# Earlier starting turns for three groups of cross-attention and spline scores inside a delta-rule loop

## The chip, the core and the metric

The kernel runs on one core of a Trainium2 chip. A core has a matrix engine (TensorE, "PE" in the profile, with its weight loads as "PEld"), three elementwise engines (VectorE "DVE", ScalarE "ACT", GpSimd "POOL"), a queue that issues transfers (SyncE "SP") and 16 transfer engines. Each engine works through its own queue in order; a program's semaphores tie the queues together. The metric is the device time of one execution in microseconds, and the figure quoted for a kernel is the median of its runs.

## What is computed

The reference is a decoder of four blocks, each made of a mixing layer, a cross-attention and a feed-forward layer, with a layer norm after every one of the twelve. The input `x` has 16 sequences of 128 tokens with 256 features. Only the first block matters here. Cut to what is needed:

```python
# layer 0: gated delta rule, 16 heads of 128; S is the state of a head
err = S @ k_t - v_t
S   = a_t * S - b_t * outer(err, k_t)
o_t = S @ q_t                      # then norm, gate, projection Wo
x = _layernorm(x + o @ Wo)

# layer 1: attention over a context, with an additive mask
x = _layernorm(x + softmax(q @ k.T / 16 + mask) @ v)

# layer 2: a spline for each token, chosen by scores of signs
xf = layernorm(x) * gamma + beta
cluster_scores = sign(xf) @ cluster_sigs.T        # best cluster, then best tile in it
tile_idx = argmax(where(in_cluster, tile_scores, -inf))
tile_min, tile_max = min / max over ALL tokens that chose a tile
x = _layernorm(x + x + spline(xf[tile_idx], tile_min, tile_max))
```

Layers 1 and 2 work on each sequence by itself, except for the last step of layer 2, which needs the extremes over all tokens. In the kernel the attention of layer 1 is taken over the tokens of `x` itself with the mask added, in line with how the reference calls it.

## The kernel before

The 16 sequences form four groups of four (`NG = 4`, a group is g = 0 to 3). A copy of `x` with features on the partitions (`xT`) and one with tokens on them (`X`) stay on the chip.

The delta rule (`s0`, from line 564) is computed in a chunked form, one unit for one head of one group, so 64 units, u = 16 g + h. A unit has two generators: `s0_inverse` (A: projections of k and q, taps of a short convolution, the decay matrix, the inverse of a triangular matrix by many 32 x 32 matmuls) and `s0_values` (B: projections of v and the gate, the output of the head, its norm, its share of the output projection). `weave` (line 299) interleaves them by hand: in turn n it walks through a fixed list of entries, and an entry (A, lag) or (B, lag) runs the next piece of unit n - lag. Two entries of the list, (C, 0), run the next piece of a third generator, `extra`. They stand seventh and thirteenth of the list, ahead of the entry that projects k and q for the turn's own unit. There are 64 units and the largest lag is 9, so there are turns 0 to 72. From turn 64 on fewer and fewer units are left and the turns get shorter. While this runs, every compute instruction is held to the order in which the program lists it on its engine (`Ordered`, line 312); transfers on SP are not.

A group is finished by unit 16 g + 15. Its output projection, the addition to `X` and the norm's moments come in turn 16 g + 23, and the norm itself and the new `xT` in turn 16 g + 24 (`s0_values`, lines 941 to 955, and `finish_in_turns`). These two turns carry more work than the others; they are called finishing turns here. For group 3 they are turns 71 and 72, the last ones.

`extra` is `s12_early` (line 965). For groups 0, 1 and 2 it runs layer 1 (`s1_group`, line 977) and the scores of layer 2 (`s2_scores`, line 1065). Both yield after each piece, 13 and 13 times, so that one group takes 13 turns at two pieces a turn. `s12_early` counts pieces and holds a group back until its starting turn. The pieces of a group in order:

- two turns of q and k projections (`qk`, four pieces of two 128 x 512 matmuls), one turn of the v projection (two pieces)
- scores with the mask (`sc`, VectorE) and the exponentials (ScalarE), then the transposes of the weights and the product with v, the addition to `X` and layer 1's norm
- `s2_scores`, nearly without TensorE: moments, `xfsg` (normalised features and signs, 128 x 1024, on VectorE, ScalarE and GpSimd), the reductions `ts`, `cs`, `best`, `oh`, `xs`, and the running extremes `run`

When the weave is over, `s0` runs whatever `extra` still has (lines 651 and 652). Then `s12_late` (line 1145) does layer 1 and the scores for group 3, and the rest of layer 2 for all groups. That part is not held to program order.

Two facts tie the groups together. The buffers of these pieces exist once: `wide` (line 981 and line 1069) holds `qk` first and `xfsg` after, so that a group's `qk` can be written only when `xs` of the group before has been read. And `mask` exists once, so that a group's mask is loaded after `sc` of the group before.

Of the kernel before, what the change touches and what calls it, by code (L numbers as in the profile page):

```python
# [326 lines left out]
class Decoder:  # L327
# [637 lines left out]
    def s12_early(self, wk, w, held):  # L965

        pieces = 0
        for g, turn in enumerate((40, 56, 68)):
            while pieces < 2 * turn:
                pieces += 1  # L970
                yield
            for part in (self.s1_group(wk, w, g), self.s2_scores(wk, held, g)):
                for _ in part:
                    pieces += 1
                    yield
# [1608 lines left out]
```

## Time and profile before

| | |
|---|---|
| median of 3 runs | 3933.04 us (3927.8 to 3938.19) |
| span of the profiled execution | 3927.2 us |
| TensorE busy | 3561.2 us, 91% |
| VectorE / ScalarE / GpSimd busy | 64% / 53% / 50% |
| chain that ended last | 73% on TensorE, 12% VectorE, 6% ScalarE, 5% GpSimd |
| mean granted TensorE clock | 0.950 |

The profile gives a time for the span alone, from the first to the last instruction; it lies 5.8 us below the median of the runs and 0.6 us below their fastest. Times in the trace count from the start of the span. The delta rule with its 64 units fills the first 1370 us or so, and the end of layer 2 comes about 1490. A turn can be told in the trace by ScalarE's first pass over the k projection (`acck<-bankA`), of which there is one in each of turns 0 to 63: turn 22 starts at 431.30, turn 38 at 747.19, turn 54 at 1071.51 and turn 62 at 1241.89 by this mark. Since the two entries of `extra` stand ahead of the mark in their turn, the stretch from mark n to mark n + 1 holds the pieces of turn n + 1.

How to read such a page: a busy share says how much of the span an engine worked, not whether it set the pace. What set the pace is read from the chain of waits and from stretches of equal content that are held against each other.

### The profile page before, as it was taken

The numbers are of one execution on the slowest core, as the hardware profiler recorded it, in microseconds if no ns is written. First come the engines' busy times: TensorE is split into PE (matmuls) and PEld (weight loads), VectorE is DVE, ScalarE is ACT, GpSimd is POOL, SyncE is SP. The second block draws the span as 40 slices with busy tenths as digits, with TensorE's granted clock in tenths as the row PEclk, the third lists the DMA queues.
The fourth block names the chain that finished last, engine by engine and source line by source line (L and its number), as shares of the span: only waits on it lengthen the run. The fifth ranks groups of instructions, "written<-read, shape, count | busy, mean of one in ns | idle before, by whom it ended". The sixth has DMA issues, their size and how long they took to land.

```text
span 3927.2 us, 96527 instructions
## 1 busy us (share of the span) xinstructions
PE 3561.2 (91%) x39282; PEld 2164.1 (55%) x39282; DVE 2528.1 (64%) x5489; ACT 2076.7 (53%) x4583; POOL 1965.7 (50%) x2227
## 2 busy tenths in 40 slices
PE   6999999999999837798989998988999999999896
PEld 4666566666666524565545664665455454555453
DVE  3776667768767565566235556755666677666697
ACT  2666666666666513343115444544656565566386
POOL 1444444435434316652125552343886666676567
PEclk8999999999999968899979998998999999999898
DMA  2111111111111101100010003111111111111221
GB/s 88 35 38 37 35 37 38 36 36 37 37 35 33 37 0 47 42 12 16 1 57 30 27 24 110 52 48 46 36 42 37 36 42 36 41 38 40 74 68 33
DMA packets 120841, 156.47 MB, mean 40 GB/s; under 512 B 15632, under 2 KB 79888, under 8 KB 120016
## 3 DMA queue, kind: packets, MB, share of 16 engines
q1 hardware_dynamic: 114544, 143.59, 12.0%
q8 instruction: 311, 5.10, 0.6%
q10 hardware_dynamic: 5712, 5.19, 0.4%
q0 software_dynamic: 144, 1.52, 0.1%
q14 instruction: 130, 1.06, 0.1%
HBM read 131.64 MB, written 2.10 MB: 34 GB/s over the span
## 4 chain that ended last, share of the span: by engine, by line
PE 73%; DVE 12%; ACT 6%; POOL 5%; issue 3%; DMA 1%; SPq 0%; ACTq 0%; POOLq 0%; DVEq 0%
PE bankA L324 39%; PE bankB L324 20%; PE bankC L324 8%; PE bankA L465 3%; DVE npad L324 2%; PE bankB L465 2%; ACT accq L324 1%; ACT ot L324 1%; ACT gT L324 1%; POOL var L324 1%; DVE X L324 1%; DVE ln_st L324 1%; POOL t L324 1%; DVE t L324 0%; DVE accq L324 0%
## 5 line engine op out<-in xcount | busy, mean ns | idle before, releaser
L324 PE MATMUL bankA<-xT,wzx 128*128 128x512 f32 x1024 | 458.1, 600 | 0.0
L324 DVE SCALAR_TENSOR_TENSOR acc<-bankA,half,acc 128x508 f32<-128x508 f32 (+2 forms) x384 | 285.2, 743 | 167.2 <-ACT acc L324 158.2
L324 POOL TENSOR_TENSOR m<-m,gm 128x512 f32<-128x512 f32 x256 | 317.9, 1277 | 48.0 <-ACT m L324 48.0
L324 PEld LDWEIGHTS bankA<-xT,wzx 128*128 128x128 f32 x1024 | 190.1, 191 | 226.6 <-issue 188.4
L324 POOL TENSOR_TENSOR eb<-eb,c_tri_s 128x512 f32<-128x512 f32 x64 | 81.2, 1269 | 371.5 <-ACT eb L324 371.5
L324 POOL TENSOR_TENSOR gT<-yx,sz 128x512 f32<-128x512 f32 x128 | 160.5, 1275 | 211.4 <-DVE yx L324 211.4
L324 PE MATMUL bankA<-xT,wkq 128*128 128x512 f32 x512 | 259.1, 631 | 0.0
L324 PE MATMUL bankA<-xT,wvg 128*128 128x512 f32 x512 | 247.5, 606 | 0.1
L324 PE MATMUL bankC<-gT,wo 128*128 128x512 f32 x512 | 231.9, 596 | 2.7 <-POOL gT L324 2.7
L324 DVE TENSOR_REDUCE npad<-bankA 128x2 f32<-128x512 f32 (+1 forms) x320 | 196.9, 681 | 37.6 <-PE bankA L324 29.0
L324 ACT ACTIVATE m<-bankA 128x512 f32<-128x512 f32 x256 | 132.1, 604 | 157.4 <-PE bankA L324 157.4
L324 ACT ACTIVATE e<-bankA 128x512 f32<-128x512 f32 x320 | 165.2, 603 | 82.2 <-PE bankA L324 81.7
L324 POOL TENSOR_TENSOR sq<-sq,s 128x512 f32<-128x512 f32 x124 | 157.5, 1271 | 56.6 <-ACT s L324 51.9
L324 POOL TENSOR_SCALAR rs_ve<-o_mv 128x4 f32<-128x4 f32 x64 | 31.5, 492 | 298.9 <-DVE o_mv L324 289.6
L324 DVE SCALAR_TENSOR_TENSOR vT<-th,accv 128x512 f32<-128x512 f32 x64 | 45.4, 710 | 182.1 <-ACT th L324 182.1
L324 PEld LDWEIGHTS bankB<-y,tt 32*32 32x32 f32 x8192 | 87.5, 107 | 129.1 <-issue 93.7
L324 DVE SCALAR_TENSOR_TENSOR yx<-xs,cols,bankB 128x512 f32<-128x512 f32 x128 | 95.0, 747 | 90.2 <-PE bankB L324 84.5
L324 DVE SCALAR_TENSOR_TENSOR acck<-bankA,half_cols,acck 128x508 f32<-128x508 f32 (+2 forms) x192 | 142.5, 742 | 11.3 <-ACT acck L324 4.8
L324 PEld LDWEIGHTS bankC<-gT,wo 128*128 128x128 f32 x512 | 93.4, 192 | 98.4 <-issue 93.5
L324 DVE SCALAR_TENSOR_TENSOR accq<-bankA,half_cols,accq 128x508 f32<-128x508 f32 (+2 forms) x192 | 142.2, 740 | 4.5
L324 ACT ACTIVATE acc<-bankA,half 128x512 f32<-128x512 f32 x128 | 100.7, 786 | 80.0 <-PE bankA L324 80.0
L324 DVE SCALAR_TENSOR_TENSOR accv<-bankA,half_cols,accv 128x508 f32<-128x508 f32 (+2 forms) x192 | 140.0, 729 | 4.5
(528 smaller groups left out, 9375.9 us busy)
## 6 DMA issues: line engine op xcount, KB each, us to landing
wzx<-in_s_wzx SPq DMA_DIRECT2D x64, 512.0 KB
up<-cums SPq DMA_DIRECT2D x1152, 2.0 KB
wkq<-in_s_w SPq DMA_DIRECT2D x64, 256.0 KB
wvg<-in_s_w SPq DMA_DIRECT2D x64, 256.0 KB
wo<-in_s_wo SPq DMA_DIRECT2D x64, 128.0 KB
sw<-qraw SPq DMA_DIRECT2D x64, 128.0 KB
eo<-in_ctx_eo SPq DMA_DIRECT2D x32, 256.0 KB
e<-in_ctx_e SPq DMA_DIRECT2D x32, 256.0 KB
```

Of the source, the lines that this page charges most:

```text
L324: return lambda *a, **k: self.tc.keep_in_program_order(f(*a, **k))
L465: self.nc.tensor.matmul(out, lhsT=lhsT, rhs=rhs, start=(k == 0), stop=(k == n - 1))
```

## The change

One line of `s12_early`: the turns at which groups 0, 1 and 2 begin.

```diff
     def s12_early(self, wk, w, held):
 
         pieces = 0
-        for g, turn in enumerate((40, 56, 68)):
+        for g, turn in enumerate((26, 42, 58)):
             while pieces < 2 * turn:
                 pieces += 1
                 yield
             for part in (self.s1_group(wk, w, g), self.s2_scores(wk, held, g)):
                 for _ in part:
                     pieces += 1
                     yield
```

Before, group 0 runs in turns 40 to 52, group 1 in turns 56 to 68, and group 2 from turn 69, since group 1's pieces are not over earlier. Turns 69 to 72 hold 8 of group 2's 26 pieces, and the other 18 follow the weave. After, the groups run in turns 26 to 38, 42 to 54 and 58 to 70, all inside the weave. The first starting turn of a group lies in both kernels after the turn in which its `xT` is written (24, 40, 56). No instruction is added or taken away; the order on each queue changes.

## The prediction

> **What bounds the kernel now.** I looked first at the chain of waits (73% of the span on TensorE), then at the chain after the delta rule, then at the delta rule cut into turns. In the chain after the rule each row is one step, with its start, its length and its work:
>
> ```profile
> 1365.58 1.29 DVE X L324 x2
> ...
> 1370.44 1.69 PE bankB L324 x8
> ...
> 1390.93 2.35 POOL xfsg L324
> ...
> 1400.25 1.95 DVE xs L324
> ...
> 1402.31 1.85 ACT qk L988 x3
> ...
> 1404.21 3.95 PE bankA L465 x16
> ...
> 1408.18 0.70 DVE sc L1006
> ```
>
> The X row and the transposes after it are group 3's finish. From there to 1402 the chain is group 2's left-over pieces, one engine after another, and then group 3's `qk`, which had to wait for `xs`. The timeline has the same place with what each instruction waited for:
>
> ```profile
> 1365.81 1.95 PE L324 MATMUL bankA<-qk 128*128 128x128 f32 x16
> 1370.44 1.69 PE L324 MATMUL bankB<-c_ident,X 128*128 128x128 f32 x8 [2.68 <-DVE X L324]
> 1371.65 1.10 ACT L324 COPY xT<-bankB 128x512 f32<-128x512 f32 x2
> ...
> 1378.50 7.11 PE L465 MATMUL bankA<-xT,w 128*128 128x512 f32 x16 [1.06 <-DVE X L324]
> 1385.44 1.89 PE L465 MATMUL bankA<-w,xT 128*128 128x256 f32 x8
> 1390.42 2.58 PE L465 MATMUL bankA<-w,xT 128*128 128x256 f32 x8 [3.09 <-DVE v L996]
> ...
> 1402.31 2.42 ACT L988 ACTIVATE qk<-bankA,cols 128x512 f32<-128x512 f32 x4 [11.46 <-DVE xs L324]
> 1404.21 3.94 PE L465 MATMUL bankA<-qk 128*128 128x128 f32 x16 [11.20 <-ACT qk L988]
> ```
>
> TensorE has group 3's projections done by 1386 and sits 11.2 us for ScalarE, which sat 11.46 us for `xs`. This is what the change sets free.
>
> Inside the rule, windows from mark to mark (length, then busy time of PE, PEld, DVE, ACT, POOL, then the granted clock) show turns 22 to 25, free of pieces, and the same places one cycle later, turns 38 to 41:
>
> ```profile
> 431.30:453.04 21.74, 21.14 (x389) 12.53 (x383) 14.78 (x37) 13.98 (x33) 8.80 (x12) 0.92 0.11 34
> 453.04:479.89 26.85, 23.22 (x400) 15.03 (x400) 18.38 (x48) 13.08 (x31) 10.08 (x14) 0.88 0.10 27
> 479.89:499.74 19.85, 19.34 (x396) 12.21 (x395) 12.41 (x33) 13.00 (x31) 8.81 (x12) 0.99 0.12 36
> 499.74:517.69 17.95, 17.87 (x391) 11.60 (x386) 12.98 (x34) 12.02 (x29) 8.80 (x12) 1.00 0.14 40
> 747.19:767.45 20.26, 19.39 (x395) 12.13 (x390) 13.54 (x35) 13.98 (x33) 8.80 (x12) 1.00 0.12 35
> 767.45:791.77 24.32, 23.99 (x416) 15.39 (x411) 19.07 (x50) 14.56 (x34) 10.08 (x14) 1.00 0.12 32
> 791.77:815.10 23.33, 22.70 (x404) 13.51 (x397) 13.25 (x34) 14.25 (x33) 8.46 (x12) 1.00 0.11 31
> 815.10:836.85 21.75, 21.48 (x408) 14.67 (x402) 14.70 (x37) 12.03 (x30) 8.46 (x12) 1.00 0.11 32
> ```
>
> A turn without pieces has TensorE busy 17.87 of 17.95 us: it is the bound, and matmuls put there lengthen the turn by their own time. The finishing turn is the exception. Without pieces it took 26.85 us, with TensorE idle 3.6 us and its clock at 0.88; with group 0's first two projections in it 24.32 us at clock 1.00. Group 0 was partly free because it began there.
>
> **The change part by part.** All times are against the profiled execution.
>
> *The rule, per turn.* I take each window with pieces minus the one 16 turns earlier, 38 to 53 minus 22 to 37: -1.5 and -2.5 in the finishing windows (38, 39; the first two `qk` pieces lie in 39), then +3.5 (`qk`), +3.8 (v), +1.2 (scores), +1.6, +0.5, -0.7, and +2.5 over the last eight. So group 0 cost 324.3 - 315.9 = 8.4 us in all, but 12.4 outside the finishing windows. Group 1, windows 54 to 62 minus 22 to 30, cost 7.1; the rest of it lies past the last mark.
>
> After the change every group starts two turns behind a finishing turn. Its first pair of `qk` then stands in a full turn and costs what the second pair did, 3.5. Groups 0 and 1 cost 3.5 + 12.4 = 15.9 each. Group 2, in windows 57 to 62, costs 3.5 + 3.5 + 3.8 + 1.2 + 1.6 + 0.5 = 14.1. The finishing windows of groups 1 and 2 fall back to 21.74 and 26.85. That makes 45.9 where there was 8.4 + 7.1 = 15.5: +30.4 us.
>
> *The clock.* Part of the 21.74 and the 26.85 is the granted clock, 0.66 at 449 to 454 and 0.57 at 476 to 481; the four passes of a `wkq` projection took 3.58 and 3.62 us there, 1.99 and 1.88 one cycle later, so a drop costs 1.6 to 1.7. Between windows 5 and 62 the drops lie in windows 18, 22, 23 and 34, all free of pieces. The one in window 23 follows the finishing turn's own waits (1.2, 1.6 and 0.7 us), and I let it recur. The other kind came in 3 of 16 even windows without pieces (6 to 36), so in the finishing windows of groups 1 and 2 13/16 of 1.6 each is not paid: -2.6. Bounds: 0 (both recur twice) to -6.6 (none). Delta rule up to the last mark: **+27.8** (23.8 to 30.4).
>
> [...]
>
> *The last turns.* Turns 69 to 72 lose group 2's `qk`, v and scores: 4 x 1.88 + 2 x 1.89 us of TensorE in front of units 62 and 63. Followed along the chain (matmul with w, moments, GpSimd, ScalarE, transposes, output), unit 63's output projection at 1362.44 waited about 1.1 us for the v matmuls (GpSimd's `ot` was done at 1361.3); before that the chain through VectorE and GpSimd is as long as TensorE's. Instead turns 65 to 70 take the `s2_scores` pieces that stood in turns 63 to 68. `xs` (1.95) sits behind a GpSimd step (2.05) and ahead of the norm of unit 62. I take **-0.5** (-3 to +2).
>
> *The tail.* The 18 left-over pieces vanish from it. Group 3's `xT` copies end at 1372.75. From there: `qk` matmuls 7.11 (ScalarE's copies run beside them, `wide` being free), v 1.89 twice, scores 1.95 as group 2's at 1365.81, 0.2 for hand-overs: `sc` at 1385.8 in place of 1408.18, -22.4. One thing is late next: with group 2's matmuls gone TensorE waits from 1365.97 to 1370.44, 4.5 us, and starts cold. After a wait of 3.09 the same eight v passes took 2.58, not 1.89 (+0.7); after 11.2 the scores took 3.94, not 1.95 (+2.0). Between these I take 1.3. Bounds: 0, and all 12.8 us of matmul at half clock, +12.8. **-21.1** (-22.4 to -9.6).
>
> *Hidden.* The three mask loads move up on SP, 0.37 us each, ahead of `wkq`, `wvg` and `wo` loads. SP is free to take them (between 745 and 795 it issued 31 loads in 15.0 us of 50), and a mask is free to load once the former `sc` is done (1174.3 after 1173.6), more than ten turns ahead of its use. Group 3's mask, which was issued at 1369.4 behind stage 3's weights, now goes before them. Without that cover it would cost one landing, by about 1375, still ahead of 1385.8.
>
> **Sum:** 27.8 - 0.5 - 21.1 = +6.2 us on 3927.2, so 3933.4 for the span; the runs' median lies 5.8 above it, so **3939.2 us**, 0.16% more. The kernel's runs spread by 0.26%, so I call 0.3% (11.8 us) what can be told from no change: the forecast is no change.
>
> **The rivals.**
>
> *The pieces ride along.* The whole-cycle comparison, 8.4 us for a group, holds wherever a group begins. Then the rule grows by 8.4 (three groups at 8.4, 8.4 and 7.1 against two), and the sum is 8.4 - 0.5 - 21.1 = -13.2: 3919.8 us, faster. For it: windows 45 to 51 hold pieces at hardly any cost. Against it: those have no matmuls, and windows 40 and 41 paid 3.5 and 3.8. Chance 0.06.
>
> *Cold tail.* Group 3's `qk`, v and scores run at half clock throughout: +12.8 in place of 1.3, sum 27.8 - 0.5 - 22.4 + 12.8 = +17.7, 3951 us, slower. It decides once 6.9 of the 12.8 are paid, half of the matmuls. For it: the clock is 0.62 over 1402 to 1445. Against it: 7.11 us for 16 `qk` passes at 1378.50 is the rule's pace. Chance 0.15.
>
> *VectorE in the last turns.* `xs` behind GpSimd and two sets of extremes (1.95 + 2.05 + 2 x 1.84 = 7.7) land between the moments and the norm of units 62 and 63, where turns are 8 us long and have no slack: sum +13.9, 3947 us, slower, from 5.6 of the 7.7 on. Against it: in turns 67 and 68 the second set (1336.85 to 1338.8) ended with GpSimd's step. Chance 0.09.
>
> **How the numbers follow.** The forecast has 0.70, with its own range 3929 to 3948: 23.8 - 3 - 22.4 = -1.6 below, 30.4 + 2 - 20.4 = +12 above (22.4 less the 2.0 of the longest wait), and 3 us of spread. Inside it I put 0.60 on no change, 0.09 on slower, 0.01 on faster. The cold tail adds 0.14 to slower and 0.01 to no change, the last turns 0.07 and 0.02, the riding pieces 0.04 to faster and 0.02 to no change. That gives faster 0.05, same 0.65, slower 0.30. The range runs from 3926 to 3954, which takes in the cold tail and leaves out the riding pieces.
>
> **What would show it.** Windows 25, 26 and 27 about 21.5, 23.8 and 22.1 us, and 38 and 39 near 21 and 26 with a clock below 1. The last mark, turn 63's at 1261.97, about 28 us later. `sc` of line 1006 some 20 us after group 3's `xT` copy, not 35. I am wrong if windows 25 to 38 together grow by less than 9, if 38 and 39 stay at clock 1.00, or if the tail's projections take 14 us.

## The result and the profile after

| | before | after |
|---|---|---|
| median (13 runs each) | 3932.76 us | 3942.38 us |
| lowest to highest | 3927.42 to 3943.81 | 3937.36 to 3955.31 |
| span of the profiled execution | 3927.2 us | 3945.4 us |
| mean granted TensorE clock | 0.950 | 0.946 |
| last mark | 1262.0 | 1293.5 |
| start of stage 3, the layer after layer 2 (`wvg<-wvg,mean`, one of its first instructions) | 1491.1 | 1503.9 |

The ratio is 1.003 with a 95% interval of 1.0018 to 1.0041. The changed kernel is slower by 9.6 us in the medians where 6.2 was forecast. That is less than the 11.8 us that I had called distinguishable from no change, but the interval, 7 to 16 us, excludes zero. The profiled execution of the changed kernel lies 18.2 us above the former one, but only 12.8 of it has arisen when stage 3 begins. The other 5.4 us fall into blocks whose instructions are the same in both kernels, and the changed kernel's own runs spread by 18 us. So I compare the two traces up to stage 3 and leave the rest to the medians.

First the delta rule. The windows from mark to mark of the changed kernel (columns as shown before: length, busy time of PE, PEld, DVE, ACT, POOL, granted clock; window n lies between marks n and n + 1) for windows 23, 25 to 27, 38, 39 and 55:

```profile
451.39:477.05 25.66, 21.83 (x400) 14.00 (x395) 19.63 (x50) 13.09 (x32) 10.08 (x14) 0.94 0.10 29
...
496.92:518.92 22.00, 21.55 (x400) 13.20 (x394) 13.51 (x35) 13.28 (x32) 8.46 (x12) 1.00 0.11 32
518.92:542.82 23.90, 23.19 (x403) 13.75 (x397) 13.23 (x35) 14.24 (x33) 8.45 (x12) 1.00 0.11 30
542.82:564.83 22.01, 21.82 (x407) 14.94 (x402) 14.97 (x37) 12.02 (x29) 8.45 (x12) 1.00 0.12 34
...
763.61:784.56 20.95, 19.37 (x395) 12.21 (x399) 15.53 (x42) 14.09 (x33) 8.90 (x13) 1.00 0.11 34
784.56:811.19 26.63, 22.95 (x400) 14.70 (x395) 19.64 (x50) 13.09 (x31) 10.07 (x14) 0.89 0.10 29
...
1118.94:1145.42 26.48, 22.81 (x400) 14.69 (x400) 18.38 (x48) 13.08 (x31) 10.07 (x14) 0.89 0.10 28
```

Windows 25 to 27 now hold group 0's projections and took 22.00, 23.90 and 22.01 us, where they had taken 17.95, 20.34 and 18.27. TensorE is busy for 21.55, 23.19 and 21.82 us of them, so the matmuls added about their own length: the two pieces took 1.88 and 1.98 us in windows 25 and 26, and 1.89 and 1.99 in window 27. Window 39 has lost its two projections and became longer, 26.63 in place of 24.32, with TensorE busy 1 us less and idle 3.7 us; its clock fell from 1.00 to 0.89. Window 55 did the same (26.48 for 24.30). The timeline of TensorE inside window 39 shows how the clock is lost:

```profile
800.20 1.99 PE L324 MATMUL bankC<-ot,wo 128*128 128x512 f32 x4 [1.18 <-POOL ot L324]
...
805.00 0.88 PE L324 MATMUL bankB<-c_ident,X 128*128 128x128 f32 x4 [1.61 <-ACT y L324]
806.56 1.12 PE L324 MATMUL bankB<-c_ident,X 128*128 128x128 f32 x4 [0.68 <-ACT xT L324]
807.47 3.62 PE L324 MATMUL bankA<-xT,wkq 128*128 128x512 f32 x4
```

Three waits of 1.18, 1.61 and 0.68 us, and the four passes of `wkq` after them took 3.62 us in place of 1.88. The granted clock is 0.50 over these passes.

Then the tail. The timeline of the changed kernel, from the last two output projections to group 3's scores:

```profile
1385.76 3.48 PE L324 MATMUL bankC<-ot,wo 128*128 128x512 f32 x4
...
1393.42 3.78 PE L324 MATMUL bankC<-ot,wo 128*128 128x512 f32 x4 [2.21 <-POOL ot L324]
...
1403.75 1.97 PE L324 MATMUL bankB<-c_ident,X 128*128 128x128 f32 x8 [4.26 <-DVE X L324]
1405.76 0.58 ACT L324 COPY xT<-bankB 128x512 f32<-128x512 f32 x1 [0.27 <-PE bankB L324]
1406.39 8.63 PE L465 MATMUL bankA<-xT,w 128*128 128x512 f32 x16 [0.67 <-ACT xT L324]
1414.86 3.62 PE L465 MATMUL bankA<-w,xT 128*128 128x256 f32 x16
1418.32 1.95 PE L465 MATMUL bankA<-qk 128*128 128x128 f32 x16
1420.30 0.69 DVE L1006 SCALAR_TENSOR_TENSOR sc<-bankA,mask 128x512 f32<-128x512 f32 x1 [1.09 <-PE bankA L465]
```

Between `xT` and `sc` nothing of group 2 is left, and TensorE goes from `qk` to v to the scores without the 11.2 us pause. Only the first row is slow, 8.63 for 7.11, at a granted clock of 0.82. What is new stands above it: both output projections ran at about half pace, 3.48 and 3.78, with a granted clock of 0.55 and 0.50 over them. In the kernel before they read:

```profile
1355.88 1.88 PE L324 MATMUL bankC<-ot,wo 128*128 128x512 f32 x4
...
1362.44 1.88 PE L324 MATMUL bankC<-ot,wo 128*128 128x512 f32 x4
```

Cut at four events, in us. The last mark is turn 63's; `ot` is the last start of ScalarE's `ot`; `xT` is the end of group 3's copies; `sc` the start of group 3's line 1006. Kernels below the second row are the experiments.

| kernel | last mark | to `ot` | to `xT` | to `sc` | to stage 3 | stage 3 at |
|---|---|---|---|---|---|---|
| before | 1262.0 | 97.2 | 13.6 | 35.4 | 82.9 | 1491.1 |
| after | 1293.5 | 97.7 | 15.1 | 14.0 | 83.6 | 1503.9 |
| 1: group 0 early | 1268.3 | 102.1 | 13.5 | 35.4 | 83.2 | 1502.5 |
| 2: groups 0, 1 early | 1275.9 | 102.9 | 13.3 | 30.8 | 83.3 | 1506.2 |
| 3: one turn late | 1268.2 | 105.2 | 13.2 | 40.0 | 83.3 | 1509.9 |
| 4: double rate at the end | 1265.1 | 129.2 | 16.8 | 14.0 | 83.3 | 1508.4 |
| 5: the same, spread | 1260.3 | 129.9 | 17.5 | 14.5 | 83.2 | 1505.5 |
| 6: without group 2 | 1254.3 | 99.8 | 14.7 | 15.3 | 83.0 | 1467.2 |
| 7: finishing turns filled | 1286.6 | 100.0 | 15.0 | 15.4 | 83.4 | 1500.4 |
| 8: filled to the end | 1290.6 | 100.2 | 12.3 | 12.5 | 83.5 | 1499.0 |
| 9: two sets of buffers | 1258.9 | 101.4 | 13.5 | 21.7 | 86.1 | 1481.6 |
| 10: after, two sets | 1299.5 | 97.9 | 14.9 | 15.4 | 82.7 | 1510.4 |

Each row is one execution. Clock drops that come and go move its last mark by some us: up to turn 68 the order of the instructions is the same before and in 6 and 9, and their last marks lie 7.7 us apart (1254.3 to 1262.0); after and 10, alike in the same way, have 1293.5 and 1299.5.

### The profile page after: what moved, and what is told of

Its sections match the earlier page's. It is cut to its first block, busy times and chain, and to the rows that moved or that the text cites. A ratio compares the mean times of both kernels' runs of the same rounds, so it can differ in the third digit from the quotient of the medians.

```text
span 3945.4 us, 96514 instructions
## 1 busy us (share of the span) xinstructions
PE 3578.4 (91%) x39267; PEld 2173.1 (55%) x39282; DVE 2530.9 (64%) x5489; ACT 2076.0 (53%) x4583; POOL 1963.6 (50%) x2227
## 4 chain that ended last, share of the span: by engine, by line
PE 72%; DVE 13%; ACT 6%; POOL 5%; issue 3%; DMA 1%; SPq 0%; ACTq 0%; POOLq 0%; DVEq 0%
PE bankA L324 39%; PE bankB L324 20%; PE bankC L324 8%; PE bankA L465 4%; DVE npad L324 2%; PE bankB L465 1%; ACT accq L324 1%; DVE X L324 1%; POOL var L324 1%; ACT gT L324 1%; ACT ot L324 1%; DVE accq L324 1%; DVE acck L324 1%; DVE ln_st L324 1%; POOL t L324 1%
## 5 line engine op out<-in xcount | busy, mean ns | idle before, releaser
L324 PE MATMUL bankA<-xT,wzx 128*128 128x512 f32 x1024 | 458.0, 600 | 0.0
L324 DVE SCALAR_TENSOR_TENSOR acc<-bankA,half,acc 128x508 f32<-128x508 f32 (+2 forms) x384 | 285.3, 743 | 167.1 <-ACT acc L324 158.1
L324 POOL TENSOR_TENSOR m<-m,gm 128x512 f32<-128x512 f32 x256 | 317.9, 1278 | 47.8 <-ACT m L324 47.8
L324 PEld LDWEIGHTS bankA<-xT,wzx 128*128 128x128 f32 x1024 | 190.1, 191 | 226.6 <-issue 188.4
L324 POOL TENSOR_TENSOR eb<-eb,c_tri_s 128x512 f32<-128x512 f32 x64 | 81.2, 1268 | 384.7 <-ACT eb L324 384.7
L324 POOL TENSOR_TENSOR gT<-yx,sz 128x512 f32<-128x512 f32 x128 | 160.6, 1276 | 211.3 <-DVE yx L324 211.3
L324 PE MATMUL bankA<-xT,wkq 128*128 128x512 f32 x512 | 262.6, 638 | 0.2 <-ACT eb L324 0.2
L324 PE MATMUL bankA<-xT,wvg 128*128 128x512 f32 x512 | 248.2, 607 | 0.5 <-issue 0.5
L324 PE MATMUL bankC<-gT,wo 128*128 128x512 f32 x512 | 231.8, 596 | 2.7 <-POOL gT L324 2.7
L324 DVE TENSOR_REDUCE npad<-bankA 128x2 f32<-128x512 f32 (+1 forms) x320 | 197.1, 682 | 40.1 <-PE bankA L324 31.9
L324 ACT ACTIVATE m<-bankA 128x512 f32<-128x512 f32 x256 | 132.1, 604 | 157.4 <-PE bankA L324 157.4
L324 ACT ACTIVATE e<-bankA 128x512 f32<-128x512 f32 x320 | 165.2, 603 | 82.3 <-PE bankA L324 81.8
L324 POOL TENSOR_TENSOR sq<-sq,s 128x512 f32<-128x512 f32 x124 | 157.7, 1272 | 56.5 <-ACT s L324 51.8
L324 POOL TENSOR_SCALAR rs_ve<-o_mv 128x4 f32<-128x4 f32 x64 | 28.6, 446 | 313.5 <-DVE o_mv L324 298.7
L324 PEld LDWEIGHTS bankB<-y,tt 32*32 32x32 f32 x8192 | 87.9, 107 | 132.0 <-issue 99.6
L324 DVE SCALAR_TENSOR_TENSOR vT<-th,accv 128x512 f32<-128x512 f32 x64 | 45.1, 705 | 179.6 <-ACT th L324 179.6
L324 DVE SCALAR_TENSOR_TENSOR yx<-xs,cols,bankB 128x512 f32<-128x512 f32 x128 | 95.0, 747 | 90.1 <-PE bankB L324 84.5
L324 DVE SCALAR_TENSOR_TENSOR acck<-bankA,half_cols,acck 128x508 f32<-128x508 f32 (+2 forms) x192 | 142.6, 742 | 13.4 <-ACT acck L324 7.0
L324 PEld LDWEIGHTS bankC<-gT,wo 128*128 128x128 f32 x512 | 93.4, 192 | 98.4 <-issue 93.5
L324 DVE SCALAR_TENSOR_TENSOR accq<-bankA,half_cols,accq 128x508 f32<-128x508 f32 (+2 forms) x192 | 142.2, 741 | 4.5
L324 DVE SCALAR_TENSOR_TENSOR accv<-bankA,half_cols,accv 128x508 f32<-128x508 f32 (+2 forms) x192 | 140.1, 730 | 4.5
L324 ACT ACTIVATE acc<-bankA,half 128x512 f32<-128x512 f32 x128 | 100.6, 786 | 79.9 <-PE bankA L324 79.9
```

What stands on the lines that cost most here:

```text
L324: return lambda *a, **k: self.tc.keep_in_program_order(f(*a, **k))
```

## The experiments

My theory: a group pays for its place. Its first projections are nearly free in a finishing turn and cost their length elsewhere, and what the tail gave back was the wait behind group 2. The ratios below are against runs of the kernel before on the same chip.

**1 and 2: one and two groups early.** The change in part; the first new line is experiment 1's, the second 2's.

```diff
-        for g, turn in enumerate((40, 56, 68)):
+        for g, turn in enumerate((26, 56, 68)):
...
+        for g, turn in enumerate((26, 42, 68)):
```

> Starting turns 26, 56, 68: only group 0 moves. Theory (place): a group costs its TensorE time in full turns, and a finishing turn takes its first pair of projections nearly free; so group 0 goes from 8.4 us to about 15.9, the last mark (1261.97 before) moves by +7 to +8, windows 25 to 27 read 22.0, 23.9 and 22.0 as after the change, the stretch from the xT copy to the scores of group 3 stays at 35 us, and the time grows by 7 us. Rival (number): only how many groups lie inside the weave matters, and two lie there as before: the last mark moves by less than 2 us, the time too.

> Starting turns 26, 42, 68: groups 0 and 1 move, group 2 stays. Theory (place and tail): the last mark moves by about +18 us (the 31.6 after the change, less the 14 of group 2), the last turns get 3 to 5 us shorter without group 1's score pieces, the tail stays as before, so the time is 13 to 15 us above before and some 4 us above after: moving group 2 alone pays. Rival (the tail gives nothing of its own): taking group 2 out of the weave again gives its 14 us back, and the time is 4 us or more below after.

Moving group 0 alone: 3941.13 us, ratio 1.0021 (1.0012 to 1.0029), last mark +6.3. Groups 0 and 1: 3951.41 us, 1.0045 (1.0030 to 1.0060), last mark +13.9. So each early start moves the last mark by 6 to 8 us in these traces, and the third is the one that gives something back: with two groups moved the kernel is further from before than with all three in the medians, though the intervals of the two ratios overlap. The expectation of 18 for two was too high for this trace, and the shorter last turns did not come: 102.9 us in place of 97.2.

**3: one turn late.** All three groups one turn after the kernel before, so that their first projections just miss the finishing turn.

```diff
-        for g, turn in enumerate((40, 56, 68)):
+        for g, turn in enumerate((41, 57, 69)):
```

> Starting turns 41, 57, 69, one turn later each: no first pair in a finishing window. Theory (a finishing turn takes the first pair free): windows 38 and 39 go from 20.3 and 24.3 to 21 and 26.5, as after the change, with a clock below 1 in 39; windows 40 and 41 show two pairs of projections at 3.5 each; the last mark moves by +11 to +14 us and the time by +11 to +16, as much as the change or more, with nothing gained in the tail. Rival (the place beside a finishing turn does not matter, the extra time after the change came from the third group): the last mark moves by less than 3 us, the time too.

3948.22 us, ratio 1.0036 (1.0024 to 1.0048). Windows 39 and 55 took 25.76 and 25.87 in place of 24.32 and 24.30, as expected, but the last mark moved by only 6.2; 2.4 us of what is missing had arisen by mark 22, before any piece runs. The rest was paid later, 8 us in the last turns and 4.6 in front of `sc`, since group 2 also came later. The total is what was expected and its split is not, so it supports the place theory less sharply than 1 does.

**4 and 5: the tail's work in the last turns.** From turn 63 on four pieces in a turn, first as pairs, then with two entries further down the list, so that group 2 ends in the weave without an early start.

```diff
             if which == 2:
-                next(extra or iter(()), None)
+                for _ in range(2 if n >= 63 else 1):
+                    next(extra or iter(()), None)
```

> Starting turns 40, 56, 68 as before, but four pieces a turn from turn 63 on, so that group 2 ends inside the weave, in turns where fewer units are left. Theory: the last mark stays within 1 us of 1261.97; the last turns grow by 5 to 12 us, since TensorE had about 10 us of idle time in turns 64 to 68; the stretch from the xT copy to the scores of group 3 falls from 35 to about 14 us; in all 9 to 16 us faster than before, about 3920. Rival (the short turns have no room: VectorE and GpSimd steps land in the chain): the last turns grow by 20 us or more, and the time is no better than before.

> As e4 (four pieces a turn from turn 63 on), but the two added pieces have places of their own later in the turn's list. Theory (in e4 two pieces in a row made an engine's queue wait for the step before on another engine): last mark to last gate product (129 us in e4, 97 before) falls to 105 to 115 us, the tail stays at 14 us, and the time is 4 to 14 us below before. Rival (the amount of work in the short turns is what costs): 125 to 132 us as in e4, the time some 15 us above before.

3951.59 us, 1.0049 (1.0035 to 1.0063), and 3946.25 us, 1.0033 (1.0022 to 1.0044): my theory missed here, and the rival held. The tail gave its 21 us back, but the last turns grew from 97.2 to 129.2 and 129.9 us. Spreading the pieces made no difference to that. The last mark of experiment 4 moved by 3.2 us where I had allowed 1. The chain of waits of experiment 4, within the last turns (start, length, step; its L325 is L324 of the others):

```profile
1299.75 2.03 POOL xfsg L325
...
1301.80 1.99 DVE xs L325
1303.79 0.80 DVE o_st L325 x4
...
1306.83 0.43 DVE cand L325
...
1308.59 0.21 DVE tt L325
...
1347.07 0.70 DVE sc L325
...
1348.52 1.65 ACT sc L325 x8
```

`xs`, `cand` and `sc` are steps of pieces and `o_st` and `tt` are steps of the units. They stand in one queue. The units' steps wait behind GpSimd's `xfsg`, which `xs` waits for, and TensorE is busy for 98.17 of the 125 us from 1265 on. These waits are not the whole of it: of the 32 us by which the last turns grew, TensorE was idle for 17.6 us more (29.6 for 12.0) and busy for 14.4 more (99.6 for 85.2), at a granted clock of 0.92 where it had been 1.00. In these short turns the pieces cost time in two ways, in waits behind GpSimd and VectorE and on TensorE itself.

**6: without group 2.** The kernel before without group 2's layer 1 and scores; what later stages read of them is set to zero.

```diff
         for g, turn in enumerate((40, 56, 68)):
...
+            if g == 2:
+                continue
```

> Kernel before without group 2's pieces: layer 1 and the scores of group 2 are left out (its choice of tiles is set to zero). This prices the tail by itself. Theory (the left-over pieces were the tail's path): the last mark stays within 2 us of before, the last turns change by -3 to +2 us, and the stretch from group 3's xT copy to its scores falls from 35 to about 14 us; the time is 20 to 25 us below before. Rival (something else holds group 3 there, the stage's weights or the mask): the stretch stays above 25 us and the time falls by less than 12.

3908.19 us, ratio 0.9936 (0.9919 to 0.9953), 24 us less. From `xT` to `sc` it took 15.3 us, so most of the price of group 2 in the kernel before is the 20 us in the tail. The last mark was to stay within 2 us and came 7.6 earlier. No piece of group 2 stands ahead of it, so that is not group 2's doing: most of it lies in windows 22, 23 and 34, where the former execution had clock drops (0.92, 0.88 and 0.93) that this one had not. The experiment also shows the bargain of the change. Taken out of the tail, the group cannot be worth more than some 24 us, and it has to be paid for in the weave.

**7: finishing turns filled.** The changed kernel with matmuls whose result nobody reads in turns 24, 40 and 56: at each `extra` entry two of the size of a projection.

```diff
             while pieces < 2 * turn:
                 pieces += 1
+                if pieces in (49, 50, 81, 82, 113, 114):
+                    p = self.ps(4, 128)
+                    for k in range(2):
+                        self.mm(p, w[:, k, :128], self.xTs(k, 12, 4), k, 2)
                 yield
```

> Changed kernel with work added: two extra k-projection pieces (two 128 x 512 matmuls each, their results read by nobody) in each of the finishing turns 24, 40 and 56. Theory (TensorE waits there and its clock falls, so matmuls are free and keep the clock up): windows 23, 39 and 55 go from 25.7, 26.6 and 26.5 with a clock of 0.89 to 0.94 down to about 24.3 at clock 1.00, as with group 0's first pieces in them before; although it does more, the time is 3 to 8 us below the changed kernel. Rival (matmuls cost their time everywhere): each of the windows grows by 3.5 and the time is about 10 us above the changed kernel.

Windows 23, 39 and 55 of this kernel:

```profile
452.14:476.46 24.32, 23.85 (x415) 15.23 (x410) 19.05 (x50) 13.21 (x31) 10.08 (x14) 1.00 0.10 31
782.64:807.21 24.57, 23.96 (x416) 15.35 (x410) 19.34 (x50) 13.19 (x32) 10.09 (x14) 1.00 0.11 31
1113.13:1137.44 24.31, 23.90 (x415) 15.28 (x409) 19.04 (x50) 13.20 (x31) 10.09 (x14) 1.00 0.11 31
```

With more to do, all three are shorter: 24.32, 24.57 and 24.31, in place of 25.66, 26.63 and 26.48, and the clock stays at 1.00. In window 39, TensorE's timeline has the same spot:

```profile
799.14 1.98 PE L324 MATMUL bankA<-xT,w 128*128 128x512 f32 x4 [0.37 <-ACT v L324]
800.97 1.88 PE L324 MATMUL bankC<-ot,wo 128*128 128x512 f32 x4
803.99 1.40 PE L324 MATMUL bankB<-c_ident,X 128*128 128x128 f32 x8
805.23 1.88 PE L324 MATMUL bankA<-xT,wkq 128*128 128x512 f32 x4
```

The unread matmul stands where TensorE had waited for `ot`; the two later waits are gone too, and `wkq` takes 1.88. The advantage of a finishing turn is therefore not only idle time that a projection fills for nothing: with the projection in it the clock stays at 1.00, and the turn gets shorter by 1.3 to 2.2 us.

All rows of the table agree. With pieces or unread matmuls in them, these three windows took 24.3 to 24.8 us at clock 1.00, 17 times out of 17. With neither they took 25.7 to 26.9 us at a clock below 0.95 in 17 cases and 24.3 at 1.00 in two, window 23 of experiments 1 and 6. So the matmuls add no time to a finishing turn, and what they save is the drop. The waits by themselves do not settle whether it comes. They stand in window 23 of experiment 1 too, and its `wkq` took 1.88:

```profile
467.17 1.98 PE L324 MATMUL bankC<-ot,wo 128*128 128x512 f32 x4 [1.18 <-POOL ot L324]
...
471.97 0.66 PE L324 MATMUL bankB<-c_ident,X 128*128 128x128 f32 x4 [1.61 <-ACT y L324]
473.39 0.66 PE L324 MATMUL bankB<-c_ident,X 128*128 128x128 f32 x4 [0.77 <-ACT xT L324]
473.89 1.88 PE L324 MATMUL bankA<-xT,wkq 128*128 128x512 f32 x4
```

The total, 3941.38 us at 1.0026 (1.0015 to 1.0037), can't be told from the changed kernel's. The 3 to 8 us that I expected to gain are not shown, although stage 3 came 3.5 us earlier in the trace.

**8: filled to the end.** The same in turns 71 and 72 as well. The expectation calls experiment 7 e8.

```diff
-        for g, turn in enumerate((26, 42, 58)):
+        for g, turn in enumerate((26, 42, 58, 73)):
...
-                if pieces in (49, 50, 81, 82, 113, 114):
+                if pieces in (49, 50, 81, 82, 113, 114, 143, 145, 146):
...
+            if g == 3:
+                return
```

> As e8, with three more such unread pieces in turns 71 and 72, where TensorE waits for the last unit. Theory (cold clock in the last turns): the last output projection takes 1.9 us in place of 3.8 and the four projections of group 3 take 7.1 in place of 8.6, the time is 2 to 6 us below e8. Rival (they stand in the way on TensorE's queue): the last turns grow by 2 to 6 us and the time lies above e8.

Its timeline of TensorE at the end of the weave:

```profile
1392.93 1.98 PE L324 MATMUL bankC<-ot,wo 128*128 128x512 f32 x4 [0.49 <-POOL ot L324]
...
1403.08 7.13 PE L465 MATMUL bankA<-xT,w 128*128 128x512 f32 x16 [0.68 <-ACT xT L324]
```

The last output projection took 1.98 and group 3's `qk` 7.13, both at full pace; the output projection before the last still took 3.35. From `ot` to `xT` it took 12.3 us and from there to `sc` 12.5, in place of 15.0 and 15.4 in experiment 7, which differs by these pieces alone. From the last mark to `sc` that makes 5.5 us less. Against the changed kernel the same stretch is only 1.9 us shorter, since this execution took 2.5 us longer to `ot`. 3939.34 us, ratio 1.0008 (0.9995 to 1.0021): this version's interval takes in no change. Against the kernel before it is 7.0 us slower in the medians where the changed kernel was 9.6 and experiment 7 was 9.0, but the three intervals overlap. So the traces show that part of the loss at the end went to the clock (0.94 from 1385 to 1420, where the changed kernel has 0.76 from 1385 to 1421); how much of it shows in the medians stays open.

**9: two sets of buffers.** If the tail paid for one set of buffers, a second set should set it free without any early start. In the kernel before, group 3 takes its buffers from `k2`, the pool of the stage that follows the weave (called `wk` in `s12_late`), in place of `k12`, the pool that groups 0 to 2 use. So it no longer waits for group 2's `wide` and `mask`. The expectation names the pool wrongly, as that of the early groups; it means the same edit.

```diff
-        for part in (self.s1_group(k12, w, NG - 1), self.s2_scores(k12, held, NG - 1)):
+        for part in (self.s1_group(wk, w, NG - 1), self.s2_scores(wk, held, NG - 1)):
```

> The kernel before, in which group 3's layer 1 and scores take their buffers from the pool that groups 0 to 2 use early, so that there are buffers for group 2 and for group 3 at the same time. Theory: what the last stretch paid for group 2 was the single set of buffers, group 3 behind group 2. From group 3's xT copies to its sc it was 35.4 us; it falls to between 15 and 25 us, since the pieces of both groups now lie beside each other, and nothing is paid in the delta rule (last mark at 1262, within 8 for clock drops). Total 8 to 20 us below the kernel before. Rival (the work of group 2 on VectorE, GpSimd and ScalarE holds group 3 back whatever its buffers): the stretch stays above 30 us and the total within 5 us of the kernel before.

3920.09 us, ratio **0.9966** (0.9954 to 0.9978): 11.3 us faster than before, and the only version here that does all the work and beats both kernels. Its chain of waits around the two groups:

```profile
1382.46 1.38 DVE X L324 x4
...
1386.91 1.39 DVE xfsg L324 x4
...
1391.98 2.35 POOL xfsg L324
...
1395.50 0.68 DVE sc L1006
...
1399.70 2.05 POOL xfsg L324
1401.78 1.98 DVE xs L324
...
1404.22 0.39 DVE X L1031
1404.62 0.33 DVE cand L324
```

Rows of L324 are group 2's pieces and rows of L1006 to L1031 are group 3's. `sc` now comes 6.3 us before group 2's `xs`, where it had come 7.9 us after it (from start to start), and 21.7 us after `xT` where it had been 35.4. It does not reach the 14 of the changed kernel: in the chain, group 2's steps on VectorE and GpSimd are still there and the two groups take turns on them. 3.2 us are paid after `sc`.

**10: the same on the changed kernel.**

> The same edit on the changed kernel (26, 42, 58). There group 2 is over before the weave ends, so the buffers have nothing to set free: from group 3's xT copies to its sc 14.0 us in the changed kernel, 13 to 16 here; last mark near 1293; total within 4 us of the changed kernel, that is 5 to 13 us above the kernel before. Rival (the second set of buffers changes more than the wait, in layer 2 or after): the stretch or the stage after it moves by more than 5 us.

3947.82 us, ratio 1.0039 (1.0025 to 1.0053). From `xT` to `sc` it took 15.4 us, as expected: with group 2 gone from the tail a second set has nothing to set free. The last mark came at 1299.5, 6 us later than in the changed kernel; 3.9 of that had arisen by mark 22, before any piece runs, and the medians differ by more than I had allowed (16.4 above before, 13 expected at most), while the two intervals overlap.

## Why the prediction was right

**The price of a place.** Windows 25, 26 and 27 were to take 21.5, 23.8 and 22.1 us and took 22.00, 23.90 and 22.01; windows 25 to 38 grew by 19.9, with 9 as the bound below which I would have been wrong. The forecast for the last mark was +27.8, made of 6.2 (group 0: 15.9 less 8.4, less a clock drop of 1.3), 7.5 (group 1: 15.9 less 7.1, less 1.3) and 14.1 (group 2). Experiments 1 and 2 and the changed kernel measure these one after another: 6.3, 13.9 - 6.3 = 7.6, and 31.6 - 13.9 = 17.7. By these traces the two moves were priced rightly and the mis-sized term is group 2's. Between experiment 2 and the changed kernel windows 57 to 62 grew from 112.7 to 128.1 us, 15.5 in place of 14.1, and windows 54 and 55 by 2.2, for clock drops.

That agreement is partly luck, as the spread between executions is as large as either price. A wider look says that the rule's term as a whole was too small. From mark 22, ahead of which no order differs, to the last mark, the three executions with the former order (before, 6 and 9) take 823.8 to 830.7 us and the two with the changed one (after and 10) 862.3 and 864.4. That is 31.6 to 40.5 us more, beyond the forecast's upper bound of 30.4 in every pairing.

The near-exact prices hide errors that cancel. Windows 25 to 37 grew by 19.2, where 15.9 was forecast: 4.05, 3.56 and 3.74 for the three turns of projections (3.5, 3.5, 3.8 forecast), 2.19 for the scores (1.2 forecast) and 1.22 where the weights meet v (0.5). Against it windows 22 to 24 shrank by 2.8, since the former execution had drops there that I let recur. In experiment 1 the two parts are -4.4 in windows 22 to 24 and +10.6 from window 25 on. I had priced the pieces against windows of a single execution, and its drops made the windows without pieces too long. Window 22 kept its clock in the eleven other executions. Window 34 kept it in the five others that have no pieces there, at 19.7 us, and lost it in all six that have group 0's, at 22.1 to 22.4; the forecast had -0.3 us for these pieces.

**The clock.** 38 and 39 were to lose theirs. Window 39 did, to 0.89, window 38 did not (20.95 us at 1.00, near the 21 forecast); window 54 did (22.41 at 0.93). I had read the finishing turn's drop as a consequence of its waits. Experiment 7 bears that out in so far as the drop goes when they are filled, but experiment 1 has the waits without a drop.

**The tail** was to give 21.1 and gave 21.4, with 14.0 us from `xT` to `sc` where 14.35 was forecast and 1.5 for the cold start where 1.3 was. Experiment 6 reaches 15.3 with the group left out. One reading of the rows was loose: group 3's q and k are done by 1386, but the second half of v ends only at 1393, and the 11.2 us of TensorE's wait begin there.

**The last turns** are the other mis-sized term: -0.5 forecast and +2.0 measured (0.5 to `ot`, 1.5 from there to `xT`). I had looked for pieces that were gained or lost on the path. What came is the clock: with group 2's matmuls in turns 71 and 72 TensorE had a granted clock of 1.00 over the last two output projections, which took 1.88 us each, and without them they ran at 3.48 and 3.78 us at 0.55 and 0.50. The table's other rows agree on the last of them: 1.88 to 1.98 us in the five executions that have these matmuls (before, 1, 2, 3, 9), 3.78 in the six that have not (after, 4, 5, 6, 7, 10). Experiment 8, with unread ones in their place, has 1.98.

Together: 31.6 + 2.0 - 21.4 = +12.2 where the sum was +6.2; stage 3 is another 0.7 later. The medians say +9.6, and their interval of 7 to 16 us leaves 6.2 just outside. The mechanism was right: full turns charge a group its length, and the tail gives back the wait behind group 2. That the total came within 3.4 us of the forecast is partly luck, since the rule's term alone was 4 to 13 us short in the traces.

**The rivals.** Pieces that ride along at 8.4 a group are refuted by windows 25 to 37. The cold tail cost 1.5 of its 12.8 us and falls well short of the 6.9 from which it decides; half clock struck earlier, in the last turns (0.55 and 0.50 over the two output projections). VectorE in the last turns would have shown as 5.6 us or more before `ot`; there were 0.5. Experiments 4 and 5 show that this mechanism is real, at double the rate.

**What stays open.** Why group 0's scores cost 1 us more in turn 29 than in turn 43 of the former kernel I didn't trace. Nor did I settle why the last turns took 5 us longer with groups 0 and 1 moved (102.9). With group 0 moved (102.1) it need not be owed to the move. Windows from the last mark to `ot`, in the kernel before, experiment 1 and experiment 9, which has the order of the kernel before throughout the weave:

```profile
1261.97:1359.18 97.21, 85.19 (x1493) 54.92 (x1484) 53.92 (x161) 60.70 (x148) 40.97 (x45) 1.00 0.06 18
1268.27:1370.35 102.08, 90.05 (x1493) 57.35 (x1485) 53.99 (x161) 60.77 (x149) 41.02 (x45) 0.95 0.06 18
1258.88:1360.27 101.39, 89.36 (x1493) 56.91 (x1483) 53.98 (x161) 60.77 (x149) 41.03 (x45) 0.95 0.06 18
```

Experiment 9 is as long without any early start, and TensorE does the same work at a clock of 0.95 in place of 1.00. Why the clock falls in one execution and not in another with the same instructions stays open.

## What to carry to other kernels

Projections that were interleaved into this loop, which TensorE bounds, cost about their full length in full turns (4.05, 3.56 and 3.74 us in windows 25 to 27) and nothing in finishing turns, where TensorE waits (24.3 to 24.8 us with them, mostly 25.7 to 26.9 without). So price each place separately; an average over a whole cycle mixes a full price with a rebate. Before work is moved out of a tail, ask what makes the tail wait: here it was a single set of buffers, and a second set for one call gave 11 us, where moving the work lost 10. Before the rate of interleaved pieces is doubled, look for slack on every engine that the pieces use: at double the rate the last turns grew by 32 us here.

## What the runs showed of the hardware

The granted clock fell after short pauses: after waits of 1.18, 1.61 and 0.68 us with small matmuls between them the next 3.6 us ran at half pace (window 39 of the changed kernel, `wkq` in 3.62 us for 1.88 at a granted clock of 0.50). Waits of that size do not stand ahead of every drop: in window 22 of the kernel before, TensorE was busy 8.62 of the 9 us ahead of 449, with a longest wait of 0.30 us, and the granted clock was 0.66 over the 5 us that followed. Matmuls in the waits kept the clock up: all 17 finishing windows with pieces or unread matmuls in them have a clock of 1.00. Of the 19 with neither, 17 lost it, so the instructions alone do not decide it.

Adding matmuls shortened a turn. In the finishing turns, unread matmuls in the gaps took windows of 25.7 to 26.6 us down to 24.3 to 24.6, the length of a turn that keeps its clock, and at the end of the weave they took the last output projection from 3.78 to 1.98 us.
